# Fewer identity products, four chunks transposed in a row, readers of one bank reordered, and loads held by a memset

## The chip, the cores and the metric

The kernel runs on one core of a Trainium2 chip. The metric is the device time of one execution in microseconds (us), shown as the median of five runs. One further execution was recorded by the profiler; all start times and durations below come from that one. The engines are named as in the profile: PE is TensorE, DVE is VectorE, ACT is ScalarE, POOL is GpSimd, SP is SyncE. A matrix instruction needs weights loaded into the array first; the profile shows these loads as PEld.

## The reference

x has 2 x 1024 tokens of 512 features. It is normalised by token, and from the normalised tokens two things are computed: a linear layer whose weights are masked in blocks of 32 x 32, and a gated feed-forward layer of inner width 1792. The output is x plus the one times the silu of the other.

```python
x = L0_attn_data
xn = _layernorm(x, axis=-1)
s = _L0_attn_ref(xn, L0_attn_weight, L0_attn_mask)     # einsum('bsk,nk->bsn', xn, weight * block_mask)
g = _silu(_L0_ffn_ref(xn, ln_w, gate_w, up_w, down_w))
...
nx = x * rsqrt(mean(square(x)) + RMS_EPS) * ln_w
return einsum('bsi,hi->bsh', silu(einsum(nx, gate_w)) * einsum(nx, up_w), down_w)
...
x = x + s * g
```

Everything is in float32.

## The kernel before

**Products.** Each large product is split twice into 2 x 2 blocks and done with seven block products in place of eight, with sums and differences of the blocks ahead of them and behind them. The outer split gives seven values of q, the inner split seven values of m. An *instance* is one pair of a group of weights g and a q; it does the seven inner products m = 1, 5, 2, 6, 3, 7, 4, each of two matrix instructions of 128x512. Three PSUM banks collect them (`instance`, from L333): bank x takes m = 1, 6, 7, 4; bank y takes 5 and 3; bank z takes 2. In between, the banks' contents are saved: `seed` copies x after m = 1 (in instances 0 and 1 into the tile s1), `snap` copies y after m = 5 into s5 and x after m = 6 into s2, and `total` adds a bank to a saved tile and so ends an output: z with s1, y with s2, x (after m = 7) with s5. Only after that last `total` may m = 4 accumulate into bank x. With no earlier partial sum (instance 0, g = 0 and q = 1) `seed` and `snap` are ScalarE copies; with one (instance 1, g = 0 and q = 2) they are VectorE additions, as `total` is.

**The start.** The tokens are four blocks t of 512, each of four tiles of 128 tokens. SyncE loads the four x tiles of block 0, then the weights of group 0 (`load_a`, two tiles K = 0 and 1, L251), block 1, group 1, block 2, group 2, block 3. For a block, VectorE computes statistics by tile (`stats`, L125 and L126) and from them a scale and a shift (`factors`: L139, a square root on ScalarE at L140, L136, L137). Tiles are normalised in place in halves of 256 columns (`normalise`): tiles 0 and 1 on ScalarE (L148), tiles 2 and 3 on VectorE (L146). TensorE transposes each of the four column chunks c of a block into a PSUM bank pt, tile by tile (`transpose`, L155), and ScalarE copies the bank to memory (`evacuate`, L163). `inner_b` makes the differences that products 5, 6, 7 and 4 of q = 1 and 2 read (line L97 is the helper `add`): m = 5 is chunk 0 of block 1 less chunk 0 of block 0, m = 6 is chunk 1 of block 1 less that difference, and so on; for q = 2 with chunks 2 and 3. They read block 1's chunks out of the PSUM banks. GpSimd multiplies group 0's weights by ln_w (`scale_a`, L262) and then makes the sums of weights that products 5, 6, 3 and 7 need (`inner_a`, L97).

**Order.** The order of work is written by hand: `at(pos, fn, ...)` notes a step with a position, and all steps are issued in order of position, each to the end of its engine's queue. A group of seven products is seven positions long; `EARLY` overrides the positions of the first two instances, and `T(us)` turns microseconds into a position. Semaphores between engines follow from what each step reads and writes. Two engines that read the same PSUM bank are kept apart too: the one issued second waits for the first. In the kernel before, ScalarE's copy of chunk 1 of block 1 is issued ahead of VectorE's second difference (m = 6, q = 1), which reads the same bank.

**Two more steps of the start.** `warm` issues identity products on TensorE while nothing has been loaded; each is two matrix instructions of 128x128 (L702). And at L685 GpSimd copies one column of the first x tile into the first weight slot, so that the load into that slot, and everything behind it in SyncE's queue, is issued only after the first x tile has landed.

Of the kernel before, what the change touches and what calls it, by code (L numbers as in the profile page):

```python
# [15 lines left out]
W = 512  # L16
# [15 lines left out]
def tile_masked_linear_gated_ffn(  # L32
# [11 lines left out]
    nc = tc.nc  # L44
# [21 lines left out]
    EARLY = {}  # L66

    def at(pos, fn, *args):
        events.append((pos, len(events), fn, args))
# [5 lines left out]
    mem = big.tile([P, sum(n for _, n in RINGS), W], F32, tag="mem", name="mem")  # L75
# [5 lines left out]
    F = first_slot  # L81

    def slot(tag, name=None):
        i, n = ring[tag]
        ring[tag][0] += 1
        return mem[:, first_slot[tag] + i % n, :]
# [6 lines left out]
    def bank(tag, name):  # L93
        return ps.tile([P, W], F32, tag=tag, name=name, bufs=PSB[tag])

    def add(eng, o, a, b, op=ALU.add):
        eng.tensor_tensor(o, a, b, op)  # L97

    dve, pool, act = nc.vector, nc.gpsimd, nc.scalar
# [14 lines left out]
    xt, raw, stat = {}, {}, {}  # L114
# [13 lines left out]
    def factors(t):  # L128


        scl = small.tile([P, TT], F32, tag="scl", name=f"scl_{t}")
        nb = small.tile([P, TT], F32, tag="nb", name=f"nb_{t}")
        stat[t] = (scl, nb)

        def last():
            nc.vector.reciprocal(scl, scl)  # L136
            nc.vector.scalar_tensor_tensor(nb, agg[:, t, :, 0], -1.0, scl, ALU.mult, ALU.mult)  # L137

        return [lambda: nc.vector.tensor_scalar(scl, agg[:, t, :, 1], 1.0 + EPS, EPS * EPS, ALU.mult, ALU.add),  # L139
                lambda: nc.scalar.activation(scl, scl, AF.Sqrt), last]  # L140
# [89 lines left out]
    def operand(q, m):  # L230
        if m in (1, 2, 3):
            k, n = {1: (0, 0), 2: (1, 0), 3: (1, 1)}[m]
            if q in (1, 2, 3):
                K, Hh = {1: (0, 0), 2: (1, 0), 3: (1, 1)}[q]
                return raw[2 * K + k, 2 * Hh + n]
            return bblk[q, k, n]
        return bop[q, m]
# [89 lines left out]
    def weights(g, q, m):  # L327
        if q < 3 and m in (1, 2, 4):
            return aq[g, 0, q - 1][:, {1: 0, 2: 2, 4: 3}[m] * P :][:, :P]
        return aop[g, q][m]  # L330


    def instance(j, g, q, prior, dest, after):  # L333


        st = {}

        seeded = j > 1

        def mm(m, tag, key, first):  # L340
            if first and key not in st:
                st[key] = bank("Y" if key == "z" and j == 1 else tag, f"{key}_{j}")
            nc.tensor.matmul(st[key], weights(g, q, m), operand(q, m), start=first and not (key == "z" and seeded),  # L343
                             stop=True, skip_group_check=True)

        def seed():

            if seeded:
                st["z"] = bank("Z", f"z_{j}")
                nc.scalar.copy(st["z"], st["x"])  # L350
            else:
                st["s1"] = slot("s2" if j else "s5", f"s1_{j}")
                if prior is None:
                    nc.scalar.copy(st["s1"], st["x"])
                else:
                    add(dve, st["s1"], st["x"], prior(0))

        def snap(key, name, i):
            s = st[name] = slot(name, f"{name}_{j}")
            if prior is None:  # L360
                nc.scalar.copy(s, st[key])
            else:
                add(dve, s, st[key], prior(i))

        def total(key, name, i):
            if key == "z" and not seeded:
                name = "s1"
            if name:
                add(dve, dest(i), st[key], st[name])
            elif prior is None:  # L370
                nc.scalar.copy(dest(i), st[key])
            else:
                add(dve, dest(i), st[key], prior(i))

        at(EARLY.get((j, 0), 7 * j + 1), seed)
        for off, m, tag, first, snapshot, out in (
            (0, 1, "X", True, None, None),
            (2, 5, "Y", True, ("s5", 3), None),
            (3, 2, "Z", True, None, (None, 0)),
            (4, 6, "X", False, ("s2", 1), None),  # L380
            (6, 3, "Y", False, None, ("s2", 1)),
            (8, 7, "X", False, None, ("s5", 3)),
            (12, 4, "X", False, None, (None, 2)),
        ):
            key, pos = tag.lower(), 7 * j + off
            at(EARLY.get((j, m), pos), mm, m, tag, key, first)
            if snapshot:
                at(pos + 1, snap, key, *snapshot)
            elif out:

                pos += 2.3 if prior is None and m == 2 and seeded else 1
                if m == 2:
                    pos = EARLY.get((j, "z"), pos)
                at(pos, total, key, *out)
                after(out[1], pos)


    def group(g, where):
# [57 lines left out]
        for q in setup:  # L456
            instance(where[g, q], g, q, *setup[q])
# [126 lines left out]
    def down_instance(o, q, where_, prior, dest, after):  # L584
# [78 lines left out]
        if last_set:  # L663
            at(where_(17) + 0.1, base_of_last)
            for part, pos in zip(parts, (where_(23), where_(24), where_(25))):
# [8 lines left out]
    where = {gq: j for j, gq in enumerate(order)}  # L674
    N = len(order)
    END = 7 * N
    T = lambda us: (us - 14.0) / 0.86
    EARLY.update({(0, 1): T(10.4), (0, 2): T(11.3), (1, 1): T(12.1), (1, 2): T(13.0), (0, 0): T(11.5), (1, 0): 4.3,
                  (0, "z"): 3.26, (1, "z"): 4.9})
    SILU = 26.2  # L680
    at(T(-10), constants)
    at(T(-10), load_x, 0)
    at(T(-10), lambda: nc.scalar.dma_start(lnw_sb, ln_w))

    at(T(-10), lambda: nc.gpsimd.tensor_copy(mem[:, F["a1"], 0:1], xt[0, 0][:, 0:1]))  # L685
    for K in range(2):
        at(T(-10), load_a, 0, K)
    at(T(-10), load_x, 1)
# [6 lines left out]
    def plan(pos, step, todo):  # L695
        for i, fn in enumerate(todo):
            at(pos + step * i, fn)


    def warm(n, b):  # L700
        for _ in range(n):
            nc.tensor.matmul(b[:, :P], ident, ident, start=True, stop=True, skip_group_check=True)  # L702

    at(T(1.4), lambda: warm(26, bank("V", "idle")))
    for t, p, step in ((0, T(7.1), 0), (1, T(12.5), 0), (2, 36.0, 1.2), (3, 36.1, 1.2)):
        plan(p, step, factors(t))
    for i in range(TT):
        half = act if i < 2 else dve
        at(T(3.7 + 0.82 * i), stats, 0, i)
        at(T(9.35 + 0.82 * i), stats, 1, i)  # L710
        for h, cols in enumerate((slice(0, W // 2), slice(W // 2, W))):
            at(T(7.95 + 0.9 * h + 0.4 * (i % 2)), normalise, 0, i, half, cols)
            at(T(13.45 + 0.9 * h + 0.4 * (i % 2)), normalise, 1, i, half, cols)
        for c in range(KC):
            at(T((8.9, 9.3, 9.8, 11.0)[c] + 0.05 * i), transpose, 0, c, (2, 3, 0, 1)[i], "XYYX"[c])
            at(T((14.35, 14.8, 15.25, 16.2)[c] + 0.05 * i), transpose, 1, c, (2, 3, 0, 1)[i], "XVVV"[c])
    at(T(6.0), scale_a, 0, 0, pool)
    at(T(6.1), scale_a, 0, 1, pool)
    for c in range(KC):
        at(T((9.75, 10.3, 10.85, 12.05)[c]), evacuate, 0, c, act)  # L720
        at((5.6, T(15.6), 6.0, 3.14)[c], evacuate, 1, c, act)
    for pos, q, m, eng in ((1.1, 1, 5, dve), (1.87, 1, 6, dve), (2.56, 1, 7, dve), (3.95, 2, 5, dve), (2.7, 1, 4, pool),
                           (4.6, 2, 6, dve), (7.2, 2, 7, dve), (5.0, 2, 4, pool)):
        at(pos, inner_b, q, m, eng)
    for q in (1, 2):
        for k in (0, 1):
            for n in (0, 1):
                at(8, outer_b, q, k, n, None)
    at(2.1, scale_a, 1, 0)
    at(5.2, scale_a, 1, 1)  # L730
    for i in range(TT):
        at(14.0 + 2.5 * i, stats, 2, i)
# [28 lines left out]
    for g in range(G + 1):  # L761
        p, rest = 7 * where[g, 1], 7 * where[g, BLOCKS[0]]
# [43 lines left out]
    def D(o):  # L806
        return lambda k: free[25 * o + k] if 25 * o + k < 25 * len(DOWN) else free[25 * o + k - 1] + 1
# [6 lines left out]
    for o, q in enumerate(DOWN):  # L814
# [24 lines left out]
        for k in range(4):  # L839
            pos = END + (-6, -4.8, 2, 4)[k] if o == 0 else D(o - 1)(10) + 2.5 * k  # L840
# [84 lines left out]
```

## Time and profile before

| What | Value |
|---|---|
| median of five runs | 513.11 us (512.75 to 513.21) |
| the profiled execution | 513.09 us |
| its span, first to last instruction | 511.3 us |
| granted TensorE clock, mean | 0.998 |
| DMA | 121.59 MB, mean 238 GB/s |
| ScalarE (ACT) busy | 182.6 us (36%) |
| GpSimd (POOL) busy | 340.7 us (67%) |

A row of a view in order of time has the start and the duration in us, the engine, the line, the operation, output and input tiles, the number of instructions drawn together, and in brackets the idle time of the engine just before and what ended it. A row of instructions by form has the total busy time, the mean duration in ns, and the idle time before them. The buffer `mem` holds nearly all tiles, so rows that name it are told apart by line, engine and time. Instructions of one engine overlap by some 0.08 us in these rows.

The time from the span's end to that of the execution, 513.09 less 511.3, is 1.8 us, and lies outside the instructions.

### The profile page before, as it was taken

How to read it: one execution, taken by the hardware profiler on the slowest of the kernel's cores; microseconds unless marked ns; L12 is line 12 of the kernel's file. 1: busy time of each engine (PE TensorE's matmuls, PEld its weight loads, DVE VectorE, ACT ScalarE, POOL GpSimd, SP SyncE). 2: the span in 40 equal slices, each digit the busy share in tenths (PEclk: the TensorE clock that was granted, in tenths of full speed). 3: DMA queues.
4: the chain of work that ended last, by engine and by line, in shares of the span. 5: the costliest groups of instructions: out<-in, count | busy, mean ns of one | idle time of the engine just before them, and what ended most of it. 6: DMA issues, size and time to landing. Idle time of an engine off the chain costs nothing. (4 is left out here: it accounts for less than half of the span.)

```text
span 511.3 us, 4943 instructions
## 1 busy us (share of the span) xinstructions
PE 505.1 (99%) x1269; PEld 230.3 (45%) x1269; DVE 382.0 (75%) x590; ACT 182.6 (36%) x348; POOL 340.7 (67%) x283
## 2 busy tenths in 40 slices
PE   8999999999999999999999999999999999999997
PEld 7444454444444444444444444444444444444444
DVE  6978689876977969698696978968737645367736
ACT  4666754633526353353634433330100101001111
POOL 4622224994795968869597789976662755739960
PEclk9999999999999999999999999999999999999999
DMA  8436636369059496685948567499997699467372
GB/s 276 176 136 241 240 135 220 140 240 360 37 213 341 160 303 227 241 285 205 324 183 298 205 241 250 169 334 381 364 334 268 205 382 320 145 252 227 142 228 83
DMA packets 60460, 121.59 MB, mean 238 GB/s; under 512 B 5760, under 2 KB 13328, under 8 KB 58384
## 3 DMA queue, kind: packets, MB, share of 16 engines
q1 hardware_dynamic: 60288, 121.27, 67.0%
q8 instruction: 10, 0.16, 0.1%
q14 instruction: 18, 0.15, 0.1%
q10 hardware_dynamic: 144, 0.00, 0.0%
HBM read 75.11 MB, written 46.15 MB: 237 GB/s over the span
## 5 line engine op out<-in xcount | busy, mean ns | idle before, releaser
L97 POOL TENSOR_TENSOR mem<-mem 128x512 f32<-128x512 f32 (+4 forms) x245 | 305.3, 1268 | 134.4 <-ACT mem L264 36.5
L343 PE MATMUL x<-mem 128*128 128x512 f32 x448 | 213.6, 594 | 0.3 <-issue 0.2
L343 PEld LDWEIGHTS x<-mem 128*128 128x128 f32 x448 | 83.7, 190 | 107.6 <-issue 87.0
L97 DVE TENSOR_TENSOR mem<-x,mem 128x512 f32<-128x512 f32 x137 | 92.8, 686 | 42.0 <-PE x L343 41.0
L343 PE MATMUL y<-mem 128*128 128x512 f32 x224 | 114.5, 593 | 0.4 <-DVE mem L97 0.3
L97 DVE TENSOR_TENSOR mem<-mem 128x512 f32<-128x512 f32 (+3 forms) x60 | 75.7, 1269 | 6.8 <-PE dx L591 4.0
L591 PE MATMUL dx<-mem 128*128 128x512 f32 x174 | 78.3, 592 | 0.0
L97 DVE TENSOR_TENSOR mem<-y,mem 128x512 f32<-128x512 f32 x96 | 65.8, 686 | 9.8 <-PE y L343 8.5
L343 PEld LDWEIGHTS y<-mem 128*128 128x128 f32 x224 | 42.2, 190 | 53.1 <-issue 47.9
L350 ACT COPY z<-x 128x512 f32<-128x512 f32 x54 | 30.9, 573 | 97.8 <-PE x L343 92.1
L343 PE MATMUL z<-mem 128*128 128x512 f32 x112 | 57.2, 593 | 0.0
L591 PEld LDWEIGHTS dx<-mem 128*128 128x128 f32 x174 | 33.1, 190 | 41.6 <-issue 40.9
L591 PE MATMUL dy<-mem 128*128 128x512 f32 x98 | 44.5, 592 | 0.0
L409 ACT ACTIVATE gate<-mem 128x512 f32<-128x512 f32 x56 | 33.1, 601 | 25.5 <-DVE mem L97 21.1
L414 DVE TENSOR_TENSOR mem<-gate,mem 128x512 f32<-128x512 f32 x56 | 38.1, 683 | 5.1 <-POOL mem L97 4.3
L564 POOL TENSOR_TENSOR mem<-mem 128x512 f32<-128x512 f32 x16 | 24.7, 1551 | 15.9 <-DMA mem<-s_dram 14.9
L343 PEld LDWEIGHTS z<-mem 128*128 128x128 f32 x112 | 21.0, 190 | 24.9 <-issue 23.7
L574 ACT ACTIVATE silu<-mem 128x512 f32<-128x512 f32 x15 | 9.0, 602 | 64.6 <-DVE mem L97 48.3
L97 DVE TENSOR_TENSOR mem<-z,mem 128x512 f32<-128x512 f32 x41 | 28.1, 685 | 3.4 <-PE z L343 3.4
L591 PEld LDWEIGHTS dy<-mem 128*128 128x128 f32 x98 | 18.6, 190 | 23.4 <-issue 23.2
L97 DVE TENSOR_TENSOR mem<-dx,mem 128x512 f32<-128x512 f32 x16 | 11.0, 690 | 20.1 <-PE dx L591 20.1
L591 PE MATMUL dz<-mem 128*128 128x512 f32 x56 | 25.2, 592 | 0.0
(73 smaller groups left out, 287.6 us busy)
## 6 DMA issues: line engine op xcount, KB each, us to landing
h_dram<-mem SPq DMA_DIRECT2D x98, 256.0 KB, 2.1
mem<-h_dram SPq DMA_DIRECT2D x28, 768.0 KB, 6.1
mem<-in_gu SPq DMA_DIRECT2D x42, 256.0 KB, 4.1
acc_dram<-mem SPq DMA_DIRECT2D x8, 1024.0 KB, 4.2
mem<-acc_dram SPq DMA_DIRECT2D x8, 1024.0 KB, 5.9
mem<-in_x SPq DMA_DIRECT2D x16, 256.0 KB, 5.2
s_dram<-mem SPq DMA_DIRECT2D x16, 256.0 KB, 4.7
mem<-s_dram SPq DMA_DIRECT2D x16, 256.0 KB, 6.3
```

What stands on the lines that cost most here:

```text
L97: eng.tensor_tensor(o, a, b, op)
L343: nc.tensor.matmul(st[key], weights(g, q, m), operand(q, m), start=first and not (key == "z" and seeded), stop=True, skip_group_check=True)
L350: nc.scalar.copy(st["z"], st["x"])
L409: nc.scalar.activation(gate[key], t(), AF.Silu)
L414: nc.vector.tensor_mul(a(), gate[key], b())
L564: at_later.append(lambda: nc.gpsimd.tensor_tensor(s_tile, s_tile, rms_bc[t], ALU.mult))
L574: nc.scalar.activation(b[0][:, part], y[:, part] if source is None else source(), AF.Silu)
L591: nc.tensor.matmul(st[key], w(), b(), start=first and key != "z", stop=True, skip_group_check=True)
```

## The change

The change is confined to the first some 25 us. It does the following.

- `warm` issues 20 identity products instead of 26.
- At L685 GpSimd clears the whole first weight slot (128x512) with a memset, which waits for no load, instead of copying a column of x.
- VectorE normalises whole tiles (2 and 3 of block 0, 2 of block 1); tile 3 of block 1 and ScalarE's tiles stay in halves.
- The tiles of a chunk are transposed in another order, and all four chunks of block 0 are transposed ahead of the first product. In block 1 chunk 2 moves behind the first product of bank y, and chunk 3 behind product 6 of instance 0.
- VectorE's second difference (m = 6, q = 1) is issued ahead of ScalarE's copy of chunk 1 of block 1, and the seed of instance 0 behind that copy.
- On VectorE the total of z in instance 0 moves ahead of the third difference (m = 7), and the total of z in instance 1 ahead of the second difference of q = 2. On ScalarE the scaling of group 1's first tile moves behind the copy of y, and the copy of x in instance 0 (s2) gets a position of its own.

```diff
-                at(pos + 1, snap, key, *snapshot)
+                at(EARLY.get((j, key), pos + 1), snap, key, *snapshot)
...
-    T = lambda us: (us - 14.0) / 0.86
-    EARLY.update({(0, 1): T(10.4), (0, 2): T(11.3), (1, 1): T(12.1), (1, 2): T(13.0), (0, 0): T(11.5), (1, 0): 4.3,
-                  (0, "z"): 3.26, (1, "z"): 4.9})
+    T = lambda us: (us - 13.4) / 0.86
+    EARLY.update({(0, 1): T(10.2), (0, 2): T(11.1), (1, 1): T(12.0), (1, 2): T(12.9), (0, 0): 1.8, (1, 0): 4.3,
+                  (0, "z"): 2.5, (1, "z"): 4.6, (0, "x"): 4.5})
...
-    at(T(-10), lambda: nc.gpsimd.tensor_copy(mem[:, F["a1"], 0:1], xt[0, 0][:, 0:1]))
+    at(T(-10), lambda: nc.gpsimd.memset(mem[:, F["a1"], :], 0.0))
...
-    at(T(1.4), lambda: warm(26, bank("V", "idle")))
-    for t, p, step in ((0, T(7.1), 0), (1, T(12.5), 0), (2, 36.0, 1.2), (3, 36.1, 1.2)):
+    at(T(1.4), lambda: warm(20, bank("V", "idle")))
+    for t, p, step in ((0, T(7.1), 0), (1, T(12.2), 0), (2, 36.0, 1.2), (3, 36.1, 1.2)):
         plan(p, step, factors(t))
     for i in range(TT):
-        half = act if i < 2 else dve
         at(T(3.7 + 0.82 * i), stats, 0, i)
-        at(T(9.35 + 0.82 * i), stats, 1, i)
-        for h, cols in enumerate((slice(0, W // 2), slice(W // 2, W))):
-            at(T(7.95 + 0.9 * h + 0.4 * (i % 2)), normalise, 0, i, half, cols)
-            at(T(13.45 + 0.9 * h + 0.4 * (i % 2)), normalise, 1, i, half, cols)
+        at(T(8.9 + 0.82 * i), stats, 1, i)
+        for t, p in ((0, T(7.75)), (1, T(13.0))):
+            if i == 2 or (t, i) == (0, 3):
+                at(p + 0.6 * (i - 2), normalise, t, i, dve)
+                continue
+            for h, cols in enumerate((slice(0, W // 2), slice(W // 2, W))):
+                at(p + 1.04 * h + 0.52 * (i % 3) if i < 2 else p + 0.6 + 0.5 * h, normalise, t, i, act if i < 2 else dve, cols)
         for c in range(KC):
-            at(T((8.9, 9.3, 9.8, 11.0)[c] + 0.05 * i), transpose, 0, c, (2, 3, 0, 1)[i], "XYYX"[c])
-            at(T((14.35, 14.8, 15.25, 16.2)[c] + 0.05 * i), transpose, 1, c, (2, 3, 0, 1)[i], "XVVV"[c])
+            at(T((8.85, 9.3, 9.75, 9.95)[c] + 0.05 * i), transpose, 0, c, ((2, 0, 1, 3), (2, 3, 0, 1))[c // 2][i], "XYYX"[c])
+            at((T(14.0), T(14.3), 2.1, 4.05)[c] + 0.01 * i, transpose, 1, c, ((0, 2, 1, 3), (2, 3, 0, 1))[c // 2][i], "XVVV"[c])
...
-        at(T((9.75, 10.3, 10.85, 12.05)[c]), evacuate, 0, c, act)
-        at((5.6, T(15.6), 6.0, 3.14)[c], evacuate, 1, c, act)
-    for pos, q, m, eng in ((1.1, 1, 5, dve), (1.87, 1, 6, dve), (2.56, 1, 7, dve), (3.95, 2, 5, dve), (2.7, 1, 4, pool),
-                           (4.6, 2, 6, dve), (7.2, 2, 7, dve), (5.0, 2, 4, pool)):
+        at(T((9.65, 10.2, 10.8, 11.4)[c]), evacuate, 0, c, act)
+        at((5.6, 1.75, 6.0, 4.7)[c], evacuate, 1, c, act)
+    for pos, q, m, eng in ((1.3, 1, 5, dve), (1.7, 1, 6, dve), (3.1, 1, 7, dve), (3.95, 2, 5, dve), (2.7, 1, 4, pool),
+                           (4.9, 2, 6, dve), (7.2, 2, 7, dve), (5.0, 2, 4, pool)):
...
-    at(2.1, scale_a, 1, 0)
+    at(3.05, scale_a, 1, 0)
```

## The prediction

> **What bounds the kernel now.** I read the table of busy time first. TensorE is busy 99% of the span, so the body of the kernel leaves nothing to win; only its start and its end can move.
>
> ```profile
> PE 505.1 (99%) x1269; PEld 230.3 (45%) x1269; DVE 382.0 (75%) x590; ACT 182.6 (36%) x348; POOL 340.7 (67%) x283
> ```
>
> Next, TensorE's own order of time around the last place where it stands idle.
>
> ```profile
> 19.97 1.10 PE L343 MATMUL x<-mem 128*128 128x512 f32 x2
> 21.41 1.10 PE L343 MATMUL y<-mem 128*128 128x512 f32 x2 [0.34 <-DVE mem L97]
> 22.34 1.96 PE L343 MATMUL x<-mem 128*128 128x512 f32 x4
> 24.13 1.02 PE L343 MATMUL y<-mem 128*128 128x512 f32 x2
> ```
>
> One product is two matrix instructions and starts 0.86 us after the one ahead. The list of TensorE's waits has no later one up to 30 us, so whatever moves the products at 22.34 (product 6 of instance 1) and 23.20 (22.34 plus 0.86: product 4 of instance 0) moves the end by as much. Each of these waits for VectorE (DVE). So I read VectorE's order of time.
>
> ```profile
> 7.47 0.18 DVE L136 RECIPROCAL scl<-scl 128x4 f32<-128x4 f32 x1 [0.27 <-ACT scl L140]
> 7.68 0.16 DVE L137 SCALAR_TENSOR_TENSOR nb<-agg,scl 128x4 f32<-128x4 f32 x1
> 7.88 1.76 DVE L146 TENSOR_SCALAR mem<-mem,scl,nb 128x256 f32<-128x256 f32 x4
> 9.57 0.68 DVE L125 BATCH_NORM_STATS2 st<-mem 128x6 f32<-128x512 f32 x1
> ...
> 12.88 0.38 DVE L139 TENSOR_SCALAR scl<-agg 128x4 f32<-128x4 f32 x1
> 13.54 0.18 DVE L136 RECIPROCAL scl<-scl 128x4 f32<-128x4 f32 x1 [0.27 <-ACT scl L140]
> 13.75 0.33 DVE L137 SCALAR_TENSOR_TENSOR nb<-agg,scl 128x4 f32<-128x4 f32 x1
> 14.12 1.95 DVE L146 TENSOR_SCALAR mem<-mem,scl,nb 128x256 f32<-128x256 f32 x4
> 15.99 0.68 DVE L97 TENSOR_TENSOR mem<-pt,mem 128x512 f32<-128x512 f32 x1
> 16.98 0.69 DVE L97 TENSOR_TENSOR mem<-pt,mem 128x512 f32<-128x512 f32 x1 [0.32 <-ACT mem L163]
> 17.59 0.68 DVE L97 TENSOR_TENSOR mem<-mem,pt 128x512 f32<-128x512 f32 x1
> ...
> 22.37 0.69 DVE L97 TENSOR_TENSOR mem<-x,mem 128x512 f32<-128x512 f32 x1
> 23.16 0.69 DVE L97 TENSOR_TENSOR mem<-y,mem 128x512 f32<-128x512 f32 x1
> ```
>
> From the first load's landing (3.69) to 23.06 VectorE stops only three times: twice for the square root (0.27) and once for a copy on ScalarE (0.32). The step at 22.37 reads bank x of instance 0 for its seventh product; once it has ended (23.06), product 4 may write there, at 23.20. So the start of this kernel is a chain on VectorE, and I price the change by that chain. Two views give the neighbours that slow it: VectorE's normalising by form, and GpSimd's order of time.
>
> ```profile
> L146 DVE TENSOR_SCALAR mem<-mem,scl,nb 128x256 f32<-128x256 f32 x8 | 3.7, 523 | 0.1
> L146 DVE TENSOR_SCALAR mem<-mem,scl,nb 128x512 f32<-128x512 f32 x4 | 2.2, 540 | 0.0
> ```
>
> ```profile
> 3.80 0.18 POOL L685 COPY mem<-mem 128x1 f32<-128x1 f32 x1 [1.72 <-DMA mem<-in_x]
> 7.99 3.76 POOL L262 TENSOR_SCALAR mem<-mem,lnw_sb 128x256 f32<-128x256 f32 x4 [4.01 <-DMA mem<-in_gu]
> 11.72 3.87 POOL L97 TENSOR_TENSOR mem<-mem 128x128 f32<-128x128 f32 x8
> ```
>
> A half tile costs VectorE nearly what a whole one does (523 against 540 ns), because seven of the eight halves ran while GpSimd worked; the one at 15.67, after GpSimd stopped, took 0.40.
>
> **The change, step by step on that chain** (minus is earlier).
>
> *Normalising block 0.* Four halves held VectorE from 7.88 to 9.57, 1.69. Two whole tiles alone are 2 x 0.54 less the overlap of 0.08 between neighbours in these rows: 0.92. The four halves ran 0.42, 0.48, 0.54 and 0.56 beside GpSimd, 2.00 against 4 x 0.40 alone, 1.25 times as long, so I take 1.15: -0.54. Bounds: -0.77 (no neighbour) and 0.
>
> *Loads held by a memset.* GpSimd clears the whole 128x512 slot instead of copying one column. A memset of one column took 0.10 and one of 128 columns 0.20; at 0.10 for each further 128 columns 512 take 0.5 (bounds 0.20 and 0.82). It starts behind the last memset (2.08), so SyncE, whose four issues end at 2.54, issues the first weights near 2.65 instead of 4.01, and every later load about 1.35 earlier. VectorE waits for no load after 3.69, so this wins nothing by itself. Two costs: the weights now follow the four x tiles at once. If they shared the rate evenly with the last two tiles, the last, issued at 2.11 and landing at 5.9, would come up to 0.6 later, and its statistics, at 6.12 now, up to 0.4 later; queued loads further on land in order, 0.67 apart, so I take 0. And GpSimd's scaling, which started 4.0 after the issue, starts at 6.7 to 7.4 (landing takes 3.8 to 4.3 in these rows), beside block 0's factors (7.03 to 7.85). Beside GpSimd these same two small steps took 0.38 and 0.33 in block 1, against 0.17 and 0.16: up to +0.38, down to 0. That neighbour was GpSimd's adding, beside which VectorE's halves took 0.54 to 0.63; beside scaling they took 0.42 to 0.56. So I take +0.15.
>
> *Block 1's statistics and factors.* 3.31 (9.57 to 12.88) and 1.24 (12.88 to 14.12). GpSimd's 7.6 of work now ends near 14.3 to 15.0, still over the factors: 0. Bounds: -0.39 (block 0's 0.85) and +0.1.
>
> *Block 1's normalising.* From 14.12 to the first difference at 15.99: 1.87, the four starts 0.54, 0.54, 0.47 and 0.32 apart, the last alone. Now one whole tile and two halves: 0.46 + 0.32 + 0.32 = 1.10 alone; with 0.2 for the first and 0.1 for the second beside GpSimd's adds 1.44, and 0.08 until the first chunk's fourth transpose is done: 1.52, so -0.35. Bounds -0.77 and 0.
>
> *First to second difference* (m = 5 and 6 of q = 1). VectorE no longer waits for ScalarE's copy of chunk 1, which now stands behind it: 0.99 becomes the 0.79 of another dependent pair (22.37 to 23.16): -0.20.
>
> *Second difference to what follows.* This is the wait that the change adds. VectorE's next step is now the total of z in instance 0, which reads the seed s1; ScalarE makes the seed after its copy of chunk 1, and that copy waits for the second difference. So: the difference 0.69; ScalarE starts 0.04 later (13.26 to 13.30 at the square root); copy to next copy 0.48 (17.95 to 18.43); the seed's copy 0.59; VectorE 0.03 later (16.95 to 16.98). Together 1.83, where it was 0.61: +1.22, bounds 1.15 and 1.3. Queued behind the waiting step on VectorE are the third difference, all of q = 2's, and the totals; TensorE waits for them.
>
> *The total of z in instance 1* now directly follows the sum that it reads: 0.79 for 0.60, +0.19. The other steps keep 0.60.
>
> The sum: -0.54 + 0.15 - 0.35 - 0.20 + 1.22 + 0.19 = +0.47. Product 4 of instance 0 comes at 23.67 instead of 23.20. (Products 5 and 6 of instance 1, which need z's total, come at 21.3 and 22.2, a little earlier than before, and then TensorE waits.)
>
> **Edits that I cost at nothing.** Six identity products fewer are 12 matrix instructions 0.11 apart, 1.3 us; TensorE waits instead until tiles are normalised (first transpose 8.74, the chunk's last needs 9.1). Chunk 3's four transposes ahead of the first product fill a gap of 0.4 and free TensorE near 14.3 instead of 14.5; it then waits for block 1 anyway. Without VectorE's chain as cover this would be worth 0.25. ScalarE's seed and copy leave a stretch in which it idled 0.5. The store behind SyncE's 8.6 us wait goes 0.47 later, and with it group 3's weights, which land near 30.4 and are scaled at 40.3.
>
> **Two rules of the Trainium skill.** The page "SBUF — State Buffer", section "SBUF: two separate sides", says that VectorE in its two-port mode and GpSimd take their shared port for a whole instruction and that the loser waits it out; this speaks against starting GpSimd earlier. By it a small step beside a scaling of 0.92 to 1.03 could lose that much, and the sum would be near +1.5. The rows disagree for scalings (no half took over 0.56 beside them), and the measurement decides. The page "TensorE: Matmul & The Clock Gate", section "Part 1", says that the array's clock halves after an idle window of some 3.4 us; 1.3 us is under that, and the sum would stay.
>
> **The rivals.**
>
> *The stall is paid, but GpSimd and the loads leave VectorE alone* (no slowing anywhere). For it: bn_stats is not slowed beside GpSimd (0.66 to 0.68 either way). Against: the factors and halves above were. With the low bounds -0.77, 0, -0.39, -0.77, -0.20, +1.15, +0.19 the sum is -0.8: 512.3. Faster by over 0.2% needs 0.2 more.
>
> *The earlier loads collide* (the slower side). Its place is 2.65 to 9.6: the weights delay the last x tile by 0.4, the factors lose 0.38, and the normalising of block 0 wins nothing. Against my sum that is +0.40, +0.23 and +0.54: +1.64, 514.7. It decides for "slower" once these three exceed 0.56 together. For it: every VectorE step with GpSimd beside it is longer but for bn_stats and those that read PSUM.
>
> *TensorE's clock drops in the new gap.* The first 13 identity instructions start between 1.3 and 4.1, 0.21 apart, and the next 38 between 4.3 and 8.5, 0.11 apart, although the granted clock reads 1.00 all along. If 1.3 us of idling brought that back for another 3 us, 1.5 us of work is lost, TensorE is free at 15.8 instead of 14.3, block 1's first chunk ends 1.15 later: +1.6, 514.7. Against it: no row shows a slow stretch after the 0.5 us gaps at 10.1 and 20.9.
>
> **How the numbers follow.** The profiled execution took 513.09 (span 511.3), 0.02 under the median 513.11: 513.09 + 0.47 + 0.02 = 513.6. Chances: this forecast 0.46 (0.43 of it within 0.2%, about 1.03 us, which is what a measurement of this kernel can tell from no change; 0.03 slower), the collision 0.27 (0.20 slower, 0.07 within), the clock 0.10 (slower), the quiet neighbours 0.17 (0.10 faster, 0.07 within). That makes 0.10 faster, 0.57 the same, 0.33 slower. The range 512.5 to 514.7 leaves out most of the quiet case and the far end of the two slow ones.
>
> **What would show it.** Right: in VectorE's order of time an idle stretch of about 1.1 us ahead of a step that reads z, ended by ScalarE; product 4 of instance 0 near 23.7 with an idle TensorE ahead of it; identity products ending near 7.5. Collision: block 0's factors or last statistics later than 7.03. Clock: transposes 0.21 apart. Wrong altogether: no such idle stretch on VectorE, or the gapless row of products starting before 21.

## The result, and the profile after

| Kernel | median (us) | range, executions | against before on the same chip |
|---|---|---|---|
| before | 513.18 | 512.63 to 513.95, 40 | |
| changed | 514.37 | 513.40 to 516.48, 21 | 1.0024 (1.0018 to 1.0030): 0.24% slower |

The forecast was 513.6 (512.5 to 514.7) with "within 0.2%" as the likeliest case. The time lies inside the range, 0.77 above the point, and just past the 0.2%, so the likeliest case did not come; the lower end of the interval (0.18%) still touches it. The busy time of TensorE is as before (`PE 505.5 (98%) x1257` after; twelve instructions fewer are the six identity products), so again only the start can have moved.

The execution that the profiler caught first is the longest of the 21 (516.48). Its VectorE, in order of time (start, duration, engine, line, operation, output and input, count, idle time before and what ended it):

```profile
7.38 0.69 DVE L125 BATCH_NORM_STATS2 st<-mem 128x6 f32<-128x512 f32 x1 [1.14 <-DMA mem<-in_x]
...
9.57 1.29 DVE L146 TENSOR_SCALAR mem<-mem,scl,nb 128x512 f32<-128x512 f32 x2
...
18.15 1.49 DVE L97 TENSOR_TENSOR mem<-pt,mem 128x512 f32<-128x512 f32 x2 [1.69 <-PE pt L155]
20.78 0.69 DVE L97 TENSOR_TENSOR mem<-z,mem 128x512 f32<-128x512 f32 x1 [1.14 <-ACT mem L354]
```

and its TensorE:

```profile
10.31 3.00 PE L155 MATMUL pt<-ident,mem 128*128 128x128 f32 x16 [2.60 <-DVE mem L146]
13.11 1.92 PE L343 MATMUL x<-mem 128*128 128x512 f32 x2
14.81 1.14 PE L343 MATMUL z<-mem 128*128 128x512 f32 x2
...
26.60 1.10 PE L343 MATMUL x<-mem 128*128 128x512 f32 x2 [0.44 <-DVE mem L97]
```

Three stops are new. The last statistics of block 0 wait 1.14 for a load; the first difference waits 1.69 for TensorE; the total of z waits 1.14 for ScalarE's seed (L354). TensorE itself ran slowly: the first product took 1.92 where such a row otherwise shows 1.02. Product 4 of instance 0 comes at 26.60 instead of 23.20, and the span is longer by the same 3.4. In every profile of this study the span less the start of product 4 is 488.0 to 488.1, so this one start tells what an execution takes.

As the first profile was an outlier, the unchanged kernel was profiled again (`after_again`, 514.11):

```profile
5.75 0.69 DVE L125 BATCH_NORM_STATS2 st<-mem 128x6 f32<-128x512 f32 x1 [0.38 <-DMA mem<-in_x]
...
7.49 0.25 DVE L139 TENSOR_SCALAR scl<-agg 128x4 f32<-128x4 f32 x1
8.01 0.18 DVE L136 RECIPROCAL scl<-scl 128x4 f32<-128x4 f32 x1 [0.27 <-ACT scl L140]
8.22 0.41 DVE L137 SCALAR_TENSOR_TENSOR nb<-agg,scl 128x4 f32<-128x4 f32 x1
8.67 1.29 DVE L146 TENSOR_SCALAR mem<-mem,scl,nb 128x512 f32<-128x512 f32 x2
9.88 0.68 DVE L125 BATCH_NORM_STATS2 st<-mem 128x6 f32<-128x512 f32 x1
...
13.21 0.25 DVE L139 TENSOR_SCALAR scl<-agg 128x4 f32<-128x4 f32 x1
...
14.14 1.43 DVE L146 TENSOR_SCALAR mem<-mem,scl,nb 128x512 f32<-128x512 f32 x3
15.76 1.49 DVE L97 TENSOR_TENSOR mem<-pt,mem 128x512 f32<-128x512 f32 x2 [0.19 <-PE pt L155]
18.39 0.69 DVE L97 TENSOR_TENSOR mem<-z,mem 128x512 f32<-128x512 f32 x1 [1.14 <-ACT mem L354]
...
23.38 0.68 DVE L97 TENSOR_TENSOR mem<-x,mem 128x512 f32<-128x512 f32 x1
24.16 0.69 DVE L97 TENSOR_TENSOR mem<-y,mem 128x512 f32<-128x512 f32 x1
```

```profile
24.20 1.10 PE L343 MATMUL x<-mem 128*128 128x512 f32 x2 [0.43 <-DVE mem L97]
```

This is the typical picture: the stop for ScalarE is there at the same 1.14, the late tile (here the third, in the first profile the fourth) costs less, TensorE is not slow, and product 4 comes at 24.20, 1.00 later than before.

The stop can be followed on ScalarE. First the seed's copy (L354) in the kernel before, then the copy of chunk 1 (L163) and the seed in the changed kernel (`after_again`):

```profile
11.72 0.59 ACT L354 COPY mem<-x 128x512 f32<-128x512 f32 x1 [0.27 <-PE x L343]
```

```profile
17.28 0.59 ACT L163 COPY mem<-pt 128x512 f32<-128x512 f32 x1 [1.07 <-DVE mem L97]
17.77 0.59 ACT L354 COPY mem<-x 128x512 f32<-128x512 f32 x1
```

The copy waits for VectorE's second difference, the seed comes behind it and ends at 18.36, and VectorE's total starts at 18.39.

From rows like these the chain on VectorE can be cut into stretches that follow each other without overlap. The table below holds the kernels whose chains are compared, one profile each; the first column is the start of block 0's factors (L139), the others are durations up to the next mark (us).

| Kernel | factors of block 0 start | they take | normalising 0 | statistics 1 | factors 1 | normalising 1, to first difference | to product 4 | factors 0 to product 4 |
|---|---|---|---|---|---|---|---|---|
| before | 7.03 | 0.85 | 1.69 | 3.31 | 1.24 | 1.87 | 7.21 | 16.17 |
| changed, again | 7.49 | 1.18 | 1.21 | 3.33 | 0.93 | 1.62 | 8.44 | 16.71 |
| e1 changed, copy hold | 6.99 | 0.85 | 1.21 | 3.33 | 1.34 | 1.65 | 8.44 | 16.82 |
| e2 changed, seed early | 7.25 | 1.27 | 1.21 | 3.32 | 0.95 | 1.62 | 7.59 | 15.96 |
| e4 both | 7.67 | 0.85 | 1.09 | 3.31 | 1.18 | 1.65 | 7.59 | 15.67 |
| e6 before, memset hold | 7.66 | 1.27 | 1.87 | 3.32 | 0.95 | 1.51 | 7.28 | 16.20 |
| e9 before, new normalising | 7.34 | 0.86 | 1.40 | 3.34 | 1.00 | 1.75 | 7.27 | 15.62 |
| e10 the same, x first | 7.00 | 0.85 | 1.14 | 3.31 | 1.02 | 2.01 | 7.28 | 15.61 |
| e13 the same as e10, again | 7.10 | 1.04 | 1.21 | 3.32 | 1.66 | 1.87 | 7.26 | 16.36 |

Line 2 less line 1: +0.46, +0.33, -0.48, +0.02, -0.31, -0.25, +1.23, together +1.00.

The first column has to be read with care: it scatters under one and the same hold. With the copy as the hold it runs from 6.99 to 7.68 over nine profiles (e7 7.41, e8 7.33 and e12 7.68 beside those above), with the memset from 7.25 to 8.32 over five (the first profile 8.32, e3 7.36). The middle values are 7.33 and 7.49. So the +0.46 of one pair of profiles doesn't measure the memset; only the medians of many executions can.

### The profile page after: what moved, and what is told of

Read it like the earlier page. It is cut to its first block, busy times and chain, and to the rows that moved or that the text cites. A ratio compares the mean times of both kernels' runs of the same rounds, so it can differ in the third digit from the quotient of the medians.

```text
span 514.7 us, 4914 instructions
## 1 busy us (share of the span) xinstructions
PE 505.5 (98%) x1257; PEld 230.6 (45%) x1257; DVE 381.3 (74%) x587; ACT 182.4 (35%) x348; POOL 342.0 (66%) x283
```

## The experiments

All were timed in five rounds beside the kernel before, whose median was 513.02 beside after_again, e1, e2 and e3, 513.25 beside e4 to e8, 513.32 beside e9 and e10, and 513.02 beside e12 and e13; across these groups only the distances to it are compared. An interval is about 0.5 us to either side. e1 to e4 and e8 are edits of the changed kernel; e6, e7, e9, e10, e12 and e13 are edits of the kernel before.

**after_again**: the changed kernel, no edit.

> The changed kernel once more, unchanged, for a second profile: the profiled execution in hand took 516.5, 2.1 over this kernel's median, so its lines are those of an extreme execution. Theory C (the earlier weight loads delay block 0's last x tile by an amount that differs between executions): the fourth statistics of block 0 start anywhere from 6.1 to 7.4, product 4 of instance 0 lies near 23.7 plus that delay, and the time is 513.6 plus the delay, near 514.4 where the delay is 0.8. Theory S (only the new wait of VectorE for ScalarE costs time): the fourth statistics start at 6.1 in a typical execution and product 4 still comes near 24.5.

Measured 514.06 (513.46 to 516.80, 11 executions), ratio 1.0027 (1.0015 to 1.0038). The slowdown is real, and so is the long tail. The profile fits the sum of theory C: the fourth statistics start at 6.58, 0.46 late, and product 4 at 24.20, where 23.7 plus 0.46 is 24.16. Theory S had 6.1. The next two runs show that neither theory has it alone.

**e1_copy_hold**: the hold undone.

```diff
-    at(T(-10), lambda: nc.gpsimd.memset(mem[:, F["a1"], :], 0.0))
+    at(T(-10), lambda: nc.gpsimd.tensor_copy(mem[:, F["a1"], 0:1], xt[0, 0][:, 0:1]))
```

> The changed kernel with GpSimd's copy of a column of x in place of the memset, so that the first weights are issued near 4.0 again. Theory C: the fourth statistics of block 0 start at 6.1 again in every execution, the executions spread no more than those of the kernel before (1.3 instead of 3.1), and the time falls to what the rest of my sum gives without the memset's share, 513.5 (+0.3 on the kernel before). Theory S: the memset costs nothing, and the time stays near 514.4.

Measured 513.98 (513.64 to 514.34), 1.0017 (1.0008 to 1.0026). Product 4 comes 0.4 earlier in the profile (23.81), but the median gains only 0.08: theory C had 0.3 over before, and it is 0.96. The bulk of the loss isn't the memset's. The highest of 11 is 514.34 instead of 516.80, but that the memset makes the tail isn't shown by it: e4, with the same hold, has an execution of 515.40 (see e8).

**e2_seed_early**: the seed of instance 0 again ahead of block 1's square root on ScalarE.

```diff
-    EARLY.update({..., (0, 0): 1.8, ...
+    EARLY.update({..., (0, 0): T(11.8), ...
```

> The changed kernel with the seed of instance 0 copied by ScalarE ahead of block 1's square root instead of behind its copy of chunk 1; the memset stays. My sum puts the new wait at 1.22 on the chain: if that is right, VectorE's stop of 1.1 ahead of z's total is gone and the time falls by about 1.1 to 1.2, to 513.2, with the spread of the changed kernel still there. If the wait is hidden behind something else (theory C alone), the time stays within 0.3 of the changed kernel's.

Measured 513.31 (512.57 to 514.62), 1.0006 (0.9997 to 1.0015): 0.75 of the 1.04 is gone with this one step, less than the 1.1 to 1.2 expected.

```profile
15.62 1.49 DVE L97 TENSOR_TENSOR mem<-pt,mem 128x512 f32<-128x512 f32 x2 [0.19 <-PE pt L155]
17.03 0.68 DVE L97 TENSOR_TENSOR mem<-z,mem 128x512 f32<-128x512 f32 x1
17.76 0.69 DVE L97 TENSOR_TENSOR mem<-mem,pt 128x512 f32<-128x512 f32 x1
...
20.96 0.68 DVE L97 TENSOR_TENSOR mem<-y,mem 128x512 f32<-128x512 f32 x1
21.78 0.69 DVE L97 TENSOR_TENSOR mem<-mem,pt 128x512 f32<-128x512 f32 x1
```

VectorE no longer stops ahead of the z total. But two smaller delays show: 17.03 to 17.76 and 20.96 to 21.78 are 0.73 and 0.82 where neighbours otherwise start 0.60 apart. In both the later step reads a chunk that ScalarE has just copied (its copies end at the same moments). So first difference to product 4 is still 7.59 against 7.21: the new order of readers costs 0.38 by itself, the late seed another 0.85. The prediction had put the new order at next to nothing (-0.20 and +0.19); the stop for the seed hid that.

**e3_ident26** and **e7_before_ident20**: the number of identity products put back in the changed kernel, and reduced in the one before (the same line the other way round).

```diff
-    at(T(1.4), lambda: warm(20, bank("V", "idle")))
+    at(T(1.4), lambda: warm(26, bank("V", "idle")))
```

> The changed kernel with 26 identity products again. In the profile in hand TensorE idled 2.6 ahead of the first transpose and then ran from 11.6 to 15 with instructions twice as far apart (granted clock 0.66 from 10.3 to 14.6). If that slow stretch belongs to the typical execution (theory G), 1.3 less of idling takes it away and the time falls by 0.5 to 1.0. If it comes only where the loads were very late, the median stays within 0.2 of the changed kernel's and at most its slowest executions go.

> The kernel before with one part of the change: 20 identity products instead of 26. The idle stretch of TensorE ahead of the first transposes grows by about 1.3 us. Theory G (a longer idle stretch costs TensorE's speed): the transposes after it are 0.21 us apart instead of about half of that, and the time grows by 1 or more. Theories C and S: no difference over 0.2 us.

Measured 514.08 (513.54 to 514.99) beside 514.06, and 513.15 (512.87 to 513.73) beside 513.25. Six identity products are worth nothing that the intervals show, as costed. The highest of e3's executions is 514.99, but seven are too few to say that the tail has gone (see e8).

**e4_hold_seed**: both undone.

> The changed kernel with two parts undone: the loads are held by the small GpSimd copy again, and the seed copy of instance 0 runs ahead of block 1's square root again. If both were charges laid on a change that otherwise saves (theory S for the seed, theory C for the loads), their undoing adds up: product 4 of instance 0 at about 22.7 (23.81 with the copy alone, less the 1.0 that the early seed alone gained: 24.20 to 23.21), 0.5 ahead of before's 23.20, and the time about 512.6 to 512.8. If the two overlap (the early seed leaves another wait as the last one, such as those of 0.05 to 0.2 us for ScalarE's evacuations seen with the early seed alone), product 4 stays near 23.2 and the time near 513.0 to 513.3.

Measured 513.29 (512.90 to 515.40), 1.0005 (0.9995 to 1.0014): the second of the two expectations. In the medians the two undoings roughly add up: 0.08 and 0.75 of the 1.04 over before would leave 0.21, and 0.04 is left; the intervals don't separate these. The further half microsecond, which I had read off e1's single profile, doesn't come. Block 0's factors came late (7.67) in this profile although the loads were held by the copy, and block 1's tiles landed only 0.18 ahead of their statistics (9.43 against 9.61): whatever block 0 gained over that would have waited there.

**e6_before_memset**: the memset alone.

> The kernel before with one part of the change: the loads held by the memset of GpSimd. Theory C (weights issued earlier put themselves beside the x tiles on the DMA engines): tile 3 of block 0 lands at 6.1 to 6.4 or later instead of 5.9, every step of block 0 shifts with it, the time grows by 0.3 to 0.5 and its spread with it (up to 2 us more in single executions). Theory S (only the new wait for ScalarE counts): no difference over 0.2 us.

Measured 513.71 (513.50 to 514.27), 1.0010 (1.0002 to 1.0019): +0.46, and none of 11 executions under 513.5.

```profile
5.92 0.69 DVE L125 BATCH_NORM_STATS2 st<-mem 128x6 f32<-128x512 f32 x1 [0.67 <-DMA mem<-in_x]
...
7.66 0.34 DVE L139 TENSOR_SCALAR scl<-agg 128x4 f32<-128x4 f32 x1
...
8.93 1.95 DVE L146 TENSOR_SCALAR mem<-mem,scl,nb 128x256 f32<-128x256 f32 x4
...
15.07 1.38 DVE L146 TENSOR_SCALAR mem<-mem,scl,nb 128x256 f32<-128x256 f32 x4
```

VectorE waits for tile 2; the factors of block 0 start 0.63 later and take 0.42 longer beside GpSimd, which now works from 7.50. Later steps give 0.36 back on the normalising of block 1 (1.38 instead of 1.95, GpSimd being done at 15.0) and 0.29 on its factors. From factors to product 4 the balance is nil (16.20 against 16.17), so in this profile the cost is the late tiles. That the memset costs something is shown by the median. That it costs it through late tiles fits this profile but isn't shown by it: the factors start at 7.67 and 7.68 in e4 and e12 too, with the copy as the hold. The wider spread that was expected didn't come: the 11 executions lie within 0.77.

**e8_hold_ident12**: the copy as the hold, and 12 identity products, so that TensorE idles long with the loads issued as late as in e1. Beside e1's edit it has this one:

```diff
-    at(T(1.4), lambda: warm(20, bank("V", "idle")))
+    at(T(1.4), lambda: warm(12, bank("V", "idle")))
```

> The changed kernel with the small GpSimd copy as the hold and only 12 identity products, so that TensorE idles for some 2.8 to 3.1 us ahead of the first transposes without any late load. Theory G: an idle stretch as long as that of the first profile of the changed kernel (2.6 us) brings the same slow stretch, transposes 0.21 us apart, a granted clock under 0.9 between 10.3 and 14.6, and 1.5 to 2 us more than the 513.98 with the copy alone. If the slow stretch came with the late load by some other way, the clock stays at 1.00 and the time within 0.2 of 513.98.

Measured 514.53 (514.34 to 515.84), 1.0028 (1.0016 to 1.0039): 1.28 over before, where e1 was 0.96 over. The 1.5 to 2 us expected on top of e1 are 0.32.

```profile
8.79 0.44 PE L155 MATMUL pt<-ident,mem 128*128 128x128 f32 x2 [2.23 <-DVE mem L146]
9.39 3.14 PE L155 MATMUL pt<-ident,mem 128*128 128x128 f32 x14 [0.16 <-ACT mem L148]
12.32 1.34 PE L343 MATMUL x<-mem 128*128 128x512 f32 x2
13.50 1.02 PE L343 MATMUL z<-mem 128*128 128x512 f32 x2
```

Fourteen transposes in 3.14 are 0.21 apart (0.11 otherwise), and the next product takes 1.34. The granted clock by stretch says the same (stretch, busy time, instructions, clock, DMA share, GB/s), first for this kernel, then for the first profile of the changed one:

```profile
10.30:14.60 4.30, 4.30 (x16) 0.69 1.05 398
```

```profile
10.30:14.60 4.30, 4.29 (x18) 0.66 1.05 386
```

So theory G's mechanism exists: an idle stretch of TensorE brings the half clock, here because identity products are missing (2.23 idle), in the first profile because a tile came late as well (2.60 idle). It isn't what makes the median: in `after_again`, e1, e2 and e3 the clock is 1.00 in every stretch. Of the 32 timed executions of the changed kernel three took over 516 (516.29, 516.48, 516.80), and these have the lowest mean clocks (0.996, 0.995, 0.995). The only other kernel with 20 identity products and so low a clock is e4: its longest execution, 515.40, has 0.995, with the copy as the hold. All six executions of e8 read 0.992 to 0.997. Wherever the mean clock of kernels with 26 is on record, it is 0.998 or more, e3 and e6 with the memset among them. So by these counts the tail goes with the fewer identity products at least as much as with the memset. In the first profile the two can be told apart: of the 2.40 by which its product 4 is later than in `after_again`, 0.83 is there at the factors, and 1.49 comes between block 1's normalising and the first difference, where TensorE is slow.

**e9_before_norm**: the new cut of the normalising alone.

```diff
...
+        for t, p in ((0, T(7.95)), (1, T(13.45))):
+            if i == 2 or (t, i) == (0, 3):
+                at(p + 0.6 * (i - 2), normalise, t, i, dve)
+                continue
...
```

> The kernel before with one part of the change: the new cut of the normalising (tiles 2 and 3 of block 0 and tile 2 of block 1 whole on VectorE), and nothing else. Read by stretches of VectorE: from the first normalising of block 0 to block 1's first statistics 1.1 to 1.2 instead of 1.69 (1.21 in the changed kernel), from block 1's first normalising to its first read of a bank about 1.65 instead of 1.87, all other stretches as before (first read of a bank to product 4 of instance 0: 7.21). If both savings reach the end, product 4 comes 0.7 earlier than its block-0 factors made it before (15.5 instead of 16.17 after them) and the time is about 512.5. If block 1's tiles set a floor (their loads had landed only 0.2 before their statistics in before: 9.37 against 9.57), the first saving is eaten by a wait for a load ahead of block 1's statistics, and only 0.2 to 0.4 remains: 512.8 to 513.0.

Measured 512.94 (512.65 to 513.68), 0.9996 (0.9987 to 1.0005): 0.38 below before by the medians, as expected for the case with a floor, but the interval includes no change.

```profile
8.20 1.20 DVE L146 TENSOR_SCALAR mem<-mem,scl,nb 128x512 f32<-128x512 f32 x2
9.60 0.70 DVE L125 BATCH_NORM_STATS2 st<-mem 128x6 f32<-128x512 f32 x1 [0.20 <-DMA mem<-in_x]
```

The normalising ended at 9.40, and VectorE then stood 0.20 for block 1's first tile: the floor that e4 suggested, seen at work.

**e10_norm_xfirst** and **e13_xfirst_again** (the same kernel): e9 with block 1's tiles loaded ahead of the second half of the first weights.

```diff
-    for K in range(2):
-        at(T(-10), load_a, 0, K)
+    at(T(-10), load_a, 0, 0)
     at(T(-10), load_x, 1)
+    at(T(-10), load_a, 0, 1)
```

> The same with block 1's four x tiles loaded ahead of the second half of the first weights, which puts them 0.67 (one 256 KB load) earlier in the stream. If the loads of block 1 are the floor, this frees the rest of the first saving: 0.3 to 0.6 below the run with the normalising alone, about 512.3 to 512.5. If they are not, nothing is gained, and where the later second half of the weights delays GpSimd's scalings past the third product of the first instances, it loses up to 0.5.

> The kernel with all four x tiles ahead once more, unchanged, on another chip: it should come out 0.3 to 0.5 below before again (0.999 of it) if its gain is real, and on both sides of before if not.

Measured 512.85 (512.40 to 513.48), 0.9990 (0.9981 to 0.9999), and 512.62 (512.21 to 513.29), 0.9994 (0.9985 to 1.0003): 0.47 and 0.40 below before by the medians, the largest gains of the study. The first interval just excludes no change, the second doesn't; nor do they tell these kernels from e9.

```profile
8.99 0.68 DVE L125 BATCH_NORM_STATS2 st<-mem 128x6 f32<-128x512 f32 x1
...
15.33 0.69 DVE L97 TENSOR_TENSOR mem<-pt,mem 128x512 f32<-128x512 f32 x1 [0.39 <-PE pt L155]
```

```profile
11.86 1.82 POOL L262 TENSOR_SCALAR mem<-mem,lnw_sb 128x256 f32<-128x256 f32 x2 [2.54 <-DMA mem<-in_gu]
```

The rows are from e10. The wait for block 1's tile is gone (normalising 0 to statistics 1.14 instead of 1.40), but GpSimd now stands 2.54 for the second half of the weights, the products that need it and block 1's transposes behind them come about 0.2 later on TensorE than a gapless row would, and VectorE waits 0.39 for those transposes. The floor moved from a load to TensorE's queue; the freed 0.26 was given back (15.61 against 15.62).

The second profile of the same kernel (e13, an execution of 513.29, the longest of its 11) doesn't repeat this: 16.36 from factors to product 4.

```profile
1.35 8.93 PE L702 MATMUL idle<-ident 128*128 128x128 f32 x52 [1.35 <-POOL ident masks.py:199]
10.11 1.47 PE L155 MATMUL pt<-ident,mem 128*128 128x128 f32 x12
```

```profile
13.78 0.18 DVE L136 RECIPROCAL scl<-scl 128x4 f32<-128x4 f32 x1 [0.80 <-ACT scl L140]
```

The 26 identity products end at 10.28 (8.91 in before) and block 0's transposes start at 10.11 (8.74). ScalarE copies the chunks later for it, reaches block 1's square root late, and VectorE waits 0.80 for that instead of 0.43 in e10. In e3 the identity products end at 10.12, and the first difference waits 0.47 for TensorE where `after_again` has 0.19. So 26 identity products can stand in the way; the last section says when.

**e12_norm_xsplit**: two of block 1's tiles ahead, two behind.

> The normalising alone, with block 1's first two x tiles loaded ahead of the second half of the first weights and its last two behind it. With all four ahead, block 1's statistics no longer waited, but GpSimd stood still for 2.54 us for the late half of the weights and the transposes of block 1 came late behind the products that need it. With two ahead, tile 0 of block 1 lands 0.67 earlier than with none, the statistics end at about 12.3 (12.68 with none ahead, 12.05 with four), and the late half lands early enough (about 10.4) that no product waits. Product 4 then comes 15.2 to 15.4 after the block-0 factors (15.61 and 15.62 in the two runs before), and the time is 512.5 to 512.8. If the floor were not in these loads, it stays at 512.85 to 512.95.

Measured 513.28 (512.96 to 513.89), 1.0006 (0.9997 to 1.0015): a miss. In its profile GpSimd waited 0.96 instead of 2.54 and no product waited, but tile 2 of block 0 landed at 5.92 and the factors started at 7.68; after that point nothing was won (15.62 to product 4). Why the loads of block 0 came late here isn't known.

## Why the prediction was right or wrong

- *What bounds the kernel.* Right: 488.0 to 488.1 from product 4 to the end in all profiles, and in each of them product 4 starts some 0.15 after the end of VectorE's seventh-product step on bank x.
- *Second difference to what follows, +1.22.* Right in mechanism, place and size: 16.56 to 18.39 is 1.83, with the 1.14 ended by ScalarE's L354 (`after_again`). Moving the seed back takes it away (e2): 0.85 of the stretch to product 4, 0.75 of the median.
- *First to second difference, -0.20*, and *total of z in instance 1, +0.19.* Measured -0.19 (0.80) and +0.18 (20.20 to 20.98). The three steps of the new order were foreseen as +1.21; the whole stretch to product 4 grew by 1.23.
- *Normalising, -0.54 and -0.35.* Measured -0.48 and -0.25. (The second term's parts, 1.10 and 0.2 and 0.1, add to 1.40 and not to the 1.44 stated; it should have been -0.39.) e9 shows the part alone, and also that the term was not free to reach the end: a load of block 1 stood 0.2 behind it. The prediction named no such floor, since VectorE waited for no load after 3.69 in before; it should have looked how far ahead of their readers the loads landed (9.37 against 9.57).
- *Factors of block 0, +0.15.* Measured +0.33, inside the bounds (0 to 0.38) and near their upper end: the two small steps took 0.25 and 0.41. *Block 1's factors, 0.* Measured -0.31, also inside.
- *The memset.* Its 0.5 measured 0.53, the first weights were issued at 2.69 (foreseen 2.65), and GpSimd's scaling started at 7.24 (6.7 to 7.4).
- *The last x tile, "I take 0".* This is the term that fell short most. The factors of block 0 started 0.46 later in the typical profile and 1.29 later (8.32) in the long one; the memset alone costs 0.46 in the median (e6). The bound of +0.4 on this term was too low for single executions: 1.14 of waiting in the first profile. With +0.46 and the factors' further 0.18 the sum would have been about +1.1 instead of +0.47; the other differences, -0.31 at block 1's factors the largest, bring it to the +1.00 of the profile, and the medians are 1.04 and 1.19 over before. How much of the 0.46 in the profile is the memset's and how much is scatter isn't settled: the prediction took its 5.9 and 7.03 from one profile, which was an early one.
- *The collision rival* had the right place, and its +0.40 for the tile and 0.38 for the factors were near (0.46 and 0.33). Its third part, that block 0's normalising wins nothing, was wrong. Its sign, factors later than 7.03, was no sign: six of the nine profiles with the copy as the hold show it too.
- *The clock rival* was right in mechanism and wrong in weight: by the mean clock it comes in three of 32 executions, not in the typical one. One of the three was profiled, and there a late tile lengthened the idle stretch. The argument against it (no slow stretch after 0.5) said nothing on longer stretches.

The sum alone missed by 0.77; that the time fell inside the range is owed to the range's upper end, 514.7, which is the time of the two slow rivals. What stays open is how much of the median the memset takes in the changed kernel: undoing it won 0.08 (e1) and, with the seed early, 0.25 (0.29 over before in e2, 0.04 in e4), where the memset alone cost the kernel before 0.46; the intervals don't separate these. That earlier weights also bring block 1's tiles earlier (first landing 8.41 in `after_again`, 9.02 in e1, 9.43 in e4) and so give something back is a reading of these landings, not tested by itself.

## What to carry to other kernels

When a step is moved behind a wait on another engine, add up the whole round trip (last producer, the other engine's queue, its copy, the way back) before the move; here the 1.83 of that sum was measured as 1.83. For every saving on a path, look up how far ahead the next loads land: a slack of 0.2 us capped it here, and moving that load too only brought up the next wait (e10). That nobody waits for some loads doesn't make it free to issue them earlier: in e6 the ones already in flight seem to have paid.

## What the runs showed of the hardware

- *TensorE's clock follows a grid of its own.* In the first profile of the changed kernel instructions start 0.21 apart up to 4.8, 0.11 apart up to 11.6, and 0.21 apart again (products at half their rate) up to 15.0; in e8 the marks are 6.1, 9.5 and 12.9. All are 3.4 apart or twice that, and the phase differs between executions. The Trainium skill, page "TensorE: Matmul & The Clock Gate", section "Part 1", describes a free-running window of about 3.4 us; these rows agree. The prediction's other rule from there, a whole idle window of some 3.4, doesn't hold here: in the two slow cases 2.1 and 2.2 of the 3.4 were idle. In e2 TensorE stood 1.83, of which some 1.6 fell into one window (7.65 to 11.06 by the same count), and the clock stayed. So, by these three stretches, what counts is how much of an idle stretch falls into one window, and one of some 2 us can pass unharmed in one execution and cost a half-speed stretch of 3.4 us in another. Where between 1.6 and 2.1 the limit lies, no run shows.
- *The same phase sets when identity products end.* At the start instructions are 0.21 apart until the first mark, which lies between 4.2 and 7.4 in these 14 profiles. With a mark at 4.5 (before) 26 identity products end at 8.91, with one at 7.4 (e13) at 10.28. More of them keep TensorE busy up to the first transposes, but in a late phase they delay these; fewer leave the gap that can bring the half clock back.
- *The profile's granted clock* reads 1.00 in the first slow stretch (1.35 to 4.8), but 0.50 within the later ones (0.66 and 0.69 over the wider stretches above): at the start the spacing of instructions is the better witness.
- *Landing times scatter.* Tile 2 of block 0 landed between 4.98 and 5.92 with the copy as the hold, though its issue began at 1.63 to 1.64 each time. A single profile can't rank two kernels that differ by less.
